# Three value products later, GpSimd for a VectorE iteration, and SyncE loads reordered, in a two-layer graph kernel

## The chip, the core and the metric

The kernel runs on one core of a Trainium2 chip. The time is device microseconds of one execution; the median of 12 executions before the change is 1186.02 us. The profiles used below each show one execution.

A core has five engines with queues of their own, each working in order: TensorE (PE; its weight loads are shown apart as PEld), VectorE (DVE), ScalarE (ACT), GpSimd (POOL) and SyncE (SP, which here only issues transfers). Transfers (DMA) are issued from SP's, ACT's or POOL's queue. An instruction that reads what another engine wrote waits on a semaphore, and all that is behind it on its engine waits too.

## The reference

`x` is 4096 x 512, `adj` a sparse symmetric 4096 x 4096 matrix with ones on the diagonal. Two layers follow each other:

```python
h = max(layernorm(x), 0)
Q, K, V = h @ WQ.T, h @ WK.T, h @ WV.T             # 8 heads of 64
attn = softmax(Q K^T / 8 + Q we^T + be, masked by adj)
hard = (attn == max of the row) / 8                # only the best neighbour(s) count
x = x + hard @ V

h = max(layernorm(x), 0)
agg = (mask @ h) / degree
x = x + relu(concat(h @ W_self + b_self, agg @ W_nb + b_nb) @ W_comb + b_comb)
```

## The kernel before the change, in words

Rows are worked in 32 tiles of 128. The kernel uses that a row has few neighbours: it makes lists of them, sorts the rows by degree, and gathers neighbours' keys and values from a table `K_d` in HBM whose row holds value, key, rank, neighbour list, layer-norm numbers and x. The order of instructions inside the stages is written out by hand: each engine's queue follows the program text.

**Stage 1** (a loop over tiles `t`, lines 955 to 1016, and what follows to 1105). In turn t the loop loads x for tile t+8 and the adjacency for tile t+2 (`load_adj`, two halves of 128 x 2048 int32, in a ring of seven half tiles: four in a pool, three in unused parts of the big tile `room`). GpSimd cuts out the diagonal block of tile t+1 (`no_self`, L673 and L677). ACT turns each half into a mask (L759) and takes row sums. PE packs the masks of tile t-1 into words by 17 small matmuls into one of two PSUM buffers `pw` (`pack`, L775 and L778), makes the keys of tile t (`keys`, four pairs of matmuls, L635) and, for tiles in `EARLY_V`, its values at once. DVE scales the keys of tile t-1 (L829, written to `K_d` by POOL at L834), finds the 24 largest words of tile t-2 (`words_top`, L849 to L853; it is what sets a `pw` free), takes row statistics of tile t+7, every fourth turn makes the reciprocal deviations of four tiles (`deviations`, L795 to L801, with `newton`, three rounds of four small instructions on DVE, L537 to L540) and in between decodes words into neighbour lists (`decode`, in pieces). Values made early are copied by ACT and written by POOL (`values_out`, L845 and L846), in the turn behind their product.

Values of the other tiles (`late_v`) are made later, from `room`, where the transposed rows are kept: eleven (`BESIDE`) beside the sorting and the last decoding (`more_values`), the rest in the first turn of stage 2 (L1674 to L1683). Zeros are written in `K_d` first where values come so late (L1024), and the x columns of half the rows are copied by four HBM-to-HBM transfers (L1019). Then SP loads the query weights `wq` into the buffer that held `wk` (L1025), biases, and the weights that are to be folded.

**Stage 2** (a loop over `turns`, L1649 on) does a tile of sorted rows in each turn. POOL gathers the rows themselves (`rows`, five turns ahead; tile `km`), then for each neighbour its key (`key_gathers`). The first 14 sorted tiles are `apart`: only keys are gathered (tiles `kg`, a ring of four groups of four), and the winner's value is gathered by head later (`o<-K_d,vi`, eight issues). The other 18 are `fused`: key and value are gathered together into `room`, so all values must be in `K_d` by then. `wide` fused rows gather their own value with `km` in one issue. DVE multiplies and sums queries and keys (L1243, L1249) and picks winners. Layer 1's products, the folding of weights (`fold`) and other work go in between. The planner's table `plan` gives the turn of each later step of a row from its place in `turns`.

**Stage 3** gathers layer 1's neighbour rows, multiplies the eight densest tiles as matrices, and writes the output.

Of the kernel before, what the change touches and what calls it, by code (L numbers as in the profile page):

```python
# [529 lines left out]
    nc.vector.bn_aggr(mv, st)  # L530


def newton(nc, pool, v, r, n, steps):

    c = pool.tile([P, n], F32, tag="nw_c", name="nw_c")
    for _ in range(steps):
        nc.vector.tensor_tensor(c, r, r, ALU.mult)  # L537
        nc.vector.tensor_tensor(c, c, v, ALU.mult)
        nc.vector.tensor_scalar(c, c, -0.5, 1.5, ALU.mult, ALU.add)
        nc.vector.tensor_tensor(r, r, c, ALU.mult)  # L540


@with_exitstack
def sparse_path(
# [40 lines left out]
    bb = cp.tile([P, D], F32, tag="sbb", name="sbb")  # L585
    wp = ctx.enter_context(tc.tile_pool(name="sw", bufs=1))

    EARLY_V = list(range(1, KT - 1, 2))
    late_v = [t for t in range(KT) if t not in EARLY_V]
    RING = 3  # L590
    SOON = 5
# [4 lines left out]
    def hT(t):  # L596
# [9 lines left out]
    END_R = HALF_R + (len(late_v) - SOON) * D  # L606
    spare = [
        room[:, at : at + N // 2]
        for at in (HALF_R - N, HALF_R - N // 2, END_R)
    ]  # L610
    assert (RING + SOON) * D <= HALF_R - N and END_R + N // 2 <= KT * D

    F = room[:, 0:HALF_R].rearrange("p (c f) -> p c f", f=D)

# [22 lines left out]
    with ExitStack() as pa:  # L637
# [18 lines left out]
        def load_adj(t):  # L656
            halves = []
            for j in range(2):
                k = (2 * t + j) % 7
                if k < 4:  # L660
                    at = a3.tile([P, N // 2], I32, tag="adjt", name="adjt")
                else:
                    at = spare[k - 4].bitcast(I32)
                nc.sync.dma_start(at, adj[ts(t, P), ts(j, N // 2)])
                halves.append(at)
            st[t]["adj"] = halves
# [124 lines left out]
        def deviations(t):  # L791

            mv = st[t]["mv"]
            v = ap.tile([P, XB], F32, tag="rs_v", name="rs_v")
            nc.vector.tensor_scalar(v, mv[:, :, 1], EPS, None, ALU.add)  # L795
            g = ap.tile([P, XB], I32, tag="rs_h", name="rs_h")
            nc.vector.tensor_scalar(g, v.bitcast(I32), 1, None, ALU.logical_shift_right)
            rs = meta[:, t : t + XB, M_LN]
            nc.vector.tensor_scalar(rs.bitcast(I32), g, -1.0, float(MAGIC), ALU.mult, ALU.add)
            newton(nc, ap, v, rs, XB, 3)  # L800
            nc.vector.scalar_tensor_tensor(  # L801
                meta[:, t : t + XB, M_LN + 1], mv[:, :, 0], -1.0, rs, ALU.mult, ALU.mult
            )
# [146 lines left out]
        def decode_some(n):  # L950
            for _ in range(n):
                next(decoding, None)

        FROM_X = KT // 2
        for t in range(KT):

            on(load_x, t + 2 * XB)
            on(load_adj, t + 2)
            if t < FROM_X:
                nc.sync.dma_start(K_d[ts(t, P), D + M_X : VKX], st[t]["x"])  # L960
            if t == 3:
                nc.scalar.dma_start(beb, be.rearrange("(o d) -> o d", o=1).to_broadcast([P, 1]))
            on(no_self, t + 1)
            on(masks, t, 0)
            on(turned_copy, t)
            on(masks, t, 1)
            on(of_self, t)
            on(norm, t + 1)
            if t == KT - 1:
                l3.close()  # L970
                rk = pa.enter_context(tc.tile_pool(name="srk", bufs=1))
                one = rk.tile([P, BINS * KT], F32, tag="r_one", name="r_one")
                nc.gpsimd.memset(one, 1.0)
                degc = rk.tile([P, KT], F32, tag="degc", name="degc")
                nc.vector.tensor_tensor(degc, degs[:, :, 0], degs[:, :, 1], ALU.add)
                rank = rk.tile([P, KT], I32, tag="rank", name="rank")
                nc.vector.tensor_scalar(rank, degc, float(BINS - 1), None, ALU.min)
                nc.vector.tensor_copy(degc, rank)
                oh = rk.tile([P, BINS, KT], BF16, tag="r_oh", name="r_oh")
                nc.vector.tensor_tensor(  # L980
                    oh, degc.unsqueeze(1).to_broadcast([P, BINS, KT]), binv, ALU.is_equal
                )
                tot = rk.tile([P, BINS * KT], F32, tag="r_tot", name="r_tot")
                acc = rk.tile([P, BINS * KT], F32, tag="r_acc", name="r_acc")
                ohf = oh.rearrange("p b t -> p (b t)")
                HF = BINS * KT // 2
            on(keys_out, t - 1)
            if t - 1 in EARLY_V:
                values_out(t - 1, st[t - 1]["pv"], ap, nc.gpsimd)
            on(pack, t - 1)  # L990
            on(keys, t)
            if t in EARLY_V:
                st[t]["pv"] = values(t, psm)
            on(turned, t + 1)
            if t == KT - 1:
                pts = [psm.tile([P, HF], F32, tag="pm", name="r_pt") for k in range(2)]
                for k in range(2):
                    nc.tensor.matmul(pts[k], onesb, ohf[:, ts(k, HF)], start=True, stop=True)
                    nc.scalar.copy(tot[:, ts(k, HF)], pts[k])
                pps = [psm.tile([P, HF], F32, tag="pm", name="r_pp") for k in range(2)]  # L1000
                nc.tensor.matmul(pps[0], tri, ohf[:, ts(0, HF)], start=True, stop=True)
            if t == 1:
                pads()
            if t == 5:
                tables()
            on(words_top, t - 2)
            on(stats, t + 2 * XB - 1)
            if t % XB == 0 and t + XB < KT:
                deviations(t + XB)
            if t - 1 in BATCHES[1:]:  # L1010
                if decoding:
                    decode_some(99)
                k = BATCHES.index(t - 1)
                decoding = decode(BATCHES[k - 1], BATCHES[k] - BATCHES[k - 1])
            if decoding and t < KT - 2:
                decode_some(2 if t < 28 else 4)
        for b in range(4):
            n = (KT - FROM_X) * P // 4
            nc.sync.dma_start(  # L1019
                K_d[ds(FROM_X * P + b * n, n), D + M_X : VKX], x[ds(FROM_X * P + b * n, n), :]  # L1020
            )

        for t in late_v[SOON:]:
            nc.sync.dma_start(K_d[ts(t, P), 0:D], zero)  # L1024
        load_w("wq", wqT, "w_a")  # L1025
        nc.sync.dma_start(bb, bcomb.rearrange("(o d) -> o d", o=1).to_broadcast([P, D]))
        for b, bias in zip(bcs, (bself, bnb)):
            nc.sync.dma_start(b, bias.rearrange("(c p) -> p c", p=P))
# [10 lines left out]
        def more_values(n):  # L1039
            make_values(n - len(made))  # L1040
            for t, pv in made:

                at = END_R + len(written) % 4 * D
                written.append(values_out(t, pv, None, nc.gpsimd, room[:, at : at + D]))
            made.clear()


# [62 lines left out]
    with ExitStack() as pb:  # L1110
# [343 lines left out]
        def fold(k, i):  # L1454

            pm = psm.tile([P, D], F32, tag="pm", name="pmw")
            if i < NC:
                left = F[:, ds(2 * k * NC, NC), ts(i, P)]
            else:
                left = fbs[k].rearrange("p (c q) -> p c q", q=P)  # L1460
            project(pm, left, F[:, ds((2 * k + 1) * NC, NC), :])
            if i < NC:
                nc.scalar.copy((wS, wN)[k][:, i, :], pm)
            else:
                biased.append(pm)

# [100 lines left out]

        fused, apart = list(range(VTILE, KT)), list(range(VTILE))
        last_tiles, ahead = fused[-4:], fused[-8:-4]
        turns = [r for pair in zip(apart, ahead + fused[:-8]) for r in pair] + last_tiles  # L1570
        pos = {r: p for p, r in enumerate(turns)}

        OWN0 = (LISTV - 1) * VK
        OWNS = (KT * D - OWN0) // VKX


        wide = [r for r in fused[:-8] if pos[r] > 12]
        big = room


# [68 lines left out]
        for i in range(-5, KT):  # L1649
# [9 lines left out]
            if i == KT - 1:  # L1659
                wT = wp.tile([P, DENSE, SEG + 2], I32, tag="w_a", name="wT")  # L1660
                nc.sync.dma_start(
                    wT[:, :, 0:SEG], W_d.rearrange("r p h q -> p r (h q)")
                )
            if i == 1:
                wS = wp.tile([P, NC, D], F32, tag="w_b", name="swS")
                wN = bp.tile([P, NC, D], F32, tag="swN", name="swN", bufs=1)
            a, b = on(key_gathers, i), late(value_gathers, "value", i)
            while a or b:
# [2 lines left out]
                        gather(*g)  # L1671
                    del q[:n]
            on(rows, i + 5)
            if i == 0:  # L1674
                for k, t in enumerate(late_v):
                    vs = xp.tile([P, D], F32, tag="xo", name="vs", bufs=2)
                    w = values_out(t, values(t, psm), None, nc.sync, vs)
                    for g in beyond:
                        tc.declare_no_dep(w.ins, g.ins, reason="other columns")
                    written.append(w)  # L1680
                    if k < 4:
                        ranks(turns[0], k, k + 1)
                late_v.clear()  # L1683
            words_copy()
            late(layer1_move, "move", i)
            on(query_copy, i + 2)
# [247 lines left out]
```

## Time and profile before

| what | value |
|---|---|
| median of 12 executions | 1186.02 us (1182.03 to 1189.09) |
| the profiled execution | 1183.13 us, its span 1181.4 us |
| mean granted TensorE clock | 0.932 |
| busy in the span: PE, DVE, ACT, POOL | 87%, 85%, 46%, 59% |
| bytes moved by DMA | 347.66 MB, mean 294 GB/s |
| stage 1, to the last decode on DVE | 303.3 us |
| stage 2, to the last key gather on POOL | 869 us |
| first row gather (`km`) | 307.75 us |
| first fused row gather | 355.21 us |

A timeline row of the profile gives start and length in us, engine, source line, operation, output and input tile, shape, how many; then in brackets the idle time of the engine ahead of it and what ended it. The table by stretches gives busy us and instruction counts of each engine for a stretch of the span. A group row gives busy us and mean ns of one instruction, then the idle time ahead. "issue" is time in which the engine waited for nothing that the profile shows. Ends of matmuls are modelled, so a full PE is not PE at its peak.

### The profile page before, as it was taken

The page shows a single profiled execution, that of the slowest core. Times are in us where ns is not written, and L with a number is a line of the kernel's source. Part 1 is how long each engine was busy: PE and PEld are TensorE (multiplying, and loading weights), DVE is VectorE, ACT ScalarE, POOL GpSimd, SP SyncE. Part 2 cuts the span into 40 slices and gives each one's busy share as a digit, 9 for nine tenths or more (in the row PEclk, how much of TensorE's full clock was granted, in tenths as well). Part 3 has the DMA queues.
Part 4 walks back from the last instruction along what each step waited for, and adds up shares of the span by engine and source line. Part 5 has one row for each costly group of instructions (what it writes and reads, how often), then busy time and mean ns, then how long its engine had stood idle before and what let it go on. Part 6 is the DMA issues. An engine that isn't in the chain of part 4 may idle for free.

```text
span 1181.4 us, 11445 instructions
## 1 busy us (share of the span) xinstructions
PE 1022.2 (87%) x3078; PEld 499.6 (42%) x3079; DVE 1000.8 (85%) x1652; ACT 549.1 (46%) x1222; POOL 695.2 (59%) x829
## 2 busy tenths in 40 slices
PE   4799999999589849976778988988989999999792
PEld 2455555554234324433334444434434444444340
DVE  6357989999388899989999999999993699998894
ACT  4577777771223358565667678845462100000000
POOL 1221222223557777777777777777713777777774
PEclk9899999999799979978889888988999999999996
DMA  9999999999587769888999888998865888988973
GB/s 352 419 419 419 383 413 400 355 341 252 192 229 231 249 210 316 259 262 287 287 289 296 275 287 286 293 287 277 287 249 178 303 304 276 319 288 275 373 244 109
DMA packets 114891, 347.66 MB, mean 294 GB/s; under 512 B 21408, under 2 KB 23488, under 8 KB 106624
## 3 DMA queue, kind: packets, MB, share of 16 engines
q0 software_dynamic: 60720, 201.79, 53.0%
q1 hardware_dynamic: 49696, 144.99, 32.0%
q10 hardware_dynamic: 4400, 0.05, 0.3%
q8 instruction: 26, 0.43, 0.1%
q14 instruction: 49, 0.40, 0.1%
HBM read 287.75 MB, written 63.21 MB: 297 GB/s over the span
## 4 chain that ended last, share of the span: by engine, by line
PE 26%; DMA 22%; DVE 21%; POOL 14%; issue 10%; ACT 4%; SPq 1%; POOLq 0%; DVEq 0%; ACTq 0%
POOL room L1120 8%; PE pk L635 7%; DMA room<-K_d,sidx 6%; DVE pr L1243 6%; PE pv L635 5%; DMA room<-G_d,sidx 5%; DVE sc L1249 4%; PE pw L778 3%; PE pr L1392 3%; PE pg L635 3%; POOL o L1120 2%; DMA K_d<-s 2%; PE q L635 2%; DVE acc L1825 2%; POOL out_dram L1136 2%
## 5 line engine op out<-in xcount | busy, mean ns | idle before, releaser
L1800 PE MATMUL da<-gk,mk 128*128 128x512 f32 x512 | 223.0, 598 | 7.2 <-DVE mk L1555 6.5
L1120 POOL DMA_INDIRECT room<-G_d,sidx x174 | 169.8, 976 | 84.5 <-issue 79.6
L635 PE MATMUL q<-wq,hqT 128*128 128x512 f32 x256 | 150.9, 744 | 57.6 <-DVE pr L1243 57.6
L1249 DVE TENSOR_REDUCE sc<-pr 128x32 f32<-128x2048 f32 (+3 forms) x114 | 183.3, 1608 | 3.8
L1120 POOL DMA_INDIRECT kg<-K_d,sidx x161 | 152.8, 949 | 48.9 <-issue 40.4
L1825 DVE TENSOR_REDUCE acc<-room 128x512 f32<-128x4096 f32 (+5 forms) x23 | 152.9, 6648 | 31.1 <-DMA room<-G_d,sidx 29.5
L1800 PEld LDWEIGHTS da<-gk,mk 128*128 128x128 f32 x512 | 98.2, 192 | 132.0 <-issue 122.9
L1120 POOL DMA_INDIRECT room<-K_d,sidx x118 | 111.4, 944 | 52.4 <-issue 20.7
L635 PE MATMUL pk<-wk,room 128*128 128x512 f32 x256 | 119.9, 613 | 9.4 <-ACT room L820 9.4
L1120 POOL DMA_INDIRECT o<-K_d,vi x112 | 107.0, 955 | 34.1 <-issue 32.6
L635 PEld LDWEIGHTS q<-wq,hqT 128*128 128x128 f32 x256 | 59.2, 243 | 129.4 <-issue 77.0
L635 PE MATMUL pv<-wv,room 128*128 128x512 f32 x256 | 112.9, 592 | 0.0
L1392 PE MATMUL pr<-swS,hT 128*128 128x512 f32 x216 | 99.1, 602 | 0.0
L1243 DVE TENSOR_TENSOR pr<-q,kg 128x2048 f32<-128x2048 f32 (+3 forms) x47 | 93.3, 1985 | 6.0 <-DMA kg<-K_d,sidx 4.9
L635 PE MATMUL pg<-swN,hT 128*128 128x512 f32 x216 | 97.1, 593 | 0.0
L1243 DVE TENSOR_TENSOR pr<-q,room 128x2048 f32<-128x2048 f32 (+3 forms) x43 | 73.9, 1718 | 15.6 <-DMA room<-K_d,sidx 12.7
L759 ACT ACTIVATE mkt<-adjt,sgb 128x2048 bf16<-128x2048 int32 x37 | 74.0, 2000 | 2.6 <-POOL adjt L677 2.6
L635 PEld LDWEIGHTS pv<-wv,room 128*128 128x128 f32 x256 | 48.4, 190 | 59.8 <-issue 59.8
L635 PEld LDWEIGHTS pk<-wk,room 128*128 128x128 f32 x256 | 47.9, 197 | 59.1 <-issue 48.7
L834 POOL DMA_DIRECT2D K_d<-ks x32 | 18.9, 589 | 79.9 <-DVE ks L829 76.6
L1392 PEld LDWEIGHTS pr<-swS,hT 128*128 128x128 f32 x216 | 41.8, 194 | 56.1 <-issue 55.2
L778 PE MATMUL pw<-mkt,planes 128*128 128x256 bf16 x512 | 61.1, 273 | 0.0
(254 smaller groups left out, 1638.2 us busy)
## 6 DMA issues: line engine op xcount, KB each, us to landing
adjt<-adj_dram SPq DMA_DIRECT2D x37, 1024.0 KB, 11.3
room<-adj_dram SPq DMA_DIRECT2D x27, 1024.0 KB, 12.2
x<-X_d SPq DMA_DIRECT2D x25, 512.0 KB, 7.8
xt<-x_dram SPq DMA_DIRECT2D x32, 256.0 KB, 8.1
K_d<-ks POOLq DMA_DIRECT2D x32, 256.0 KB, 6.5
X_d<-xo SPq DMA_DIRECT2D x32, 256.0 KB, 5.7
G_d<-gs SPq DMA_DIRECT2D x32, 256.0 KB, 4.5
gk<-G_d SPq DMA_DIRECT2D x16, 512.0 KB, 5.1
```

The costliest lines, as they stand in the source:

```text
L635: nc.tensor.matmul(dst, h[:, c, :], w[:, c, :], start=(c == 0), stop=(c == NC - 1))
L759: nc.scalar.activation(mk, st[t]["adj"][j], AF.Sigmoid, bias=sgb, scale=400.0, accum_out=degs[:, t, j : j + 1],)
L778: nc.tensor.matmul(pw, planes[:, s, :], st[t]["mk"][j][:, ts(i, SEG)], start=False, stop=(s == NPL - 1),)
L834: nc.gpsimd.dma_start(K_d[ts(t, P), D : 2 * D], ks)
L1120: last[0] = nc.gpsimd.indirect_dma_start(out=dst, out_offset=None, in_=src, in_offset=bass.IndirectOffsetOnAxis(ap=idx, axis=0), element_o ...
L1136: new = nc.gpsimd.indirect_dma_start(out=dst, out_offset=bass.IndirectOffsetOnAxis(ap=perm[:, r : r + 1], axis=0), in_=src, in_offset=None,)
L1243: nc.vector.tensor_tensor(pr[:, :g, :], s["q"].unsqueeze(1).to_broadcast([P, g, D]), kk[:, :, 0:D], ALU.mult)
L1249: nc.vector.tensor_reduce(sc[:, g0 : g0 + g, :], pr[:, :g, :].rearrange("p g (h d) -> p g h d", h=H), AX.X, ALU.add,)
L1392: nc.tensor.matmul(pr, s["hT1"][:, c, :], wS[:, c, :], start=False, stop=(c == NC - 1 and mine is None and not open_))
L1800: nc.tensor.matmul(dacc[r], masks[s][:, r, h, :], keys[s][:, h, :], start=(s == 0 and h == 0), stop=(s == NPL - 1 and h == 1),)
L1825: nc.vector.tensor_reduce(acc, g[:, 0:n, :].rearrange("p n f -> p f n"), AX.X, ALU.add)
```

## The change

It has six parts in one edit.

1. `newton` takes an engine, and `deviations` gives GpSimd: its twelve small instructions in each of eight calls leave DVE and stand in POOL's queue.
2. `EARLY_V` ends at tile 23 instead of 29: tiles 25, 27 and 29 join `late_v`, which has 20 tiles now instead of 17. Eleven are still made beside the sorting, six in turn 0 of stage 2 as before, and three in turn 1. Their rows in `room` take the place of the third spare half tile.
3. The adjacency ring has therefore six half tiles.
4. `wq` is loaded ahead of the four x copies and the zeros in SP's queue (there are 15 zeros instead of 12).
5. Late values beside the sorting are copied to four buffers in the pool `srk` instead of a part of `room`.
6. The first ten turns have another order: two `apart` tiles come ahead of the first `fused` one. The buffer for one folded weight is taken a turn later, with its copy order exchanged to suit, and `wide` begins two places later (7 rows instead of 8).

```diff
-def newton(nc, pool, v, r, n, steps):
+def newton(nc, pool, v, r, n, steps, eng=None):
+    eng = eng or nc.vector
     c = pool.tile([P, n], F32, tag="nw_c", name="nw_c")
     for _ in range(steps):
-        nc.vector.tensor_tensor(c, r, r, ALU.mult)
-        nc.vector.tensor_tensor(c, c, v, ALU.mult)
-        nc.vector.tensor_scalar(c, c, -0.5, 1.5, ALU.mult, ALU.add)
-        nc.vector.tensor_tensor(r, r, c, ALU.mult)
+        eng.tensor_tensor(c, r, r, ALU.mult)
+        eng.tensor_tensor(c, c, v, ALU.mult)
+        eng.tensor_scalar(c, c, -0.5, 1.5, ALU.mult, ALU.add)
+        eng.tensor_tensor(r, r, c, ALU.mult)
...
-    EARLY_V = list(range(1, KT - 1, 2))
+    EARLY_V = list(range(1, 24, 2))
...
-        for at in (HALF_R - N, HALF_R - N // 2, END_R)
+        for at in (HALF_R - N, HALF_R - N // 2)
...
-                k = (2 * t + j) % 7
+                k = (2 * t + j) % 6
...
-            newton(nc, ap, v, rs, XB, 3)
+            newton(nc, ap, v, rs, XB, 3, nc.gpsimd)
...
+        load_w("wq", wqT, "w_a")
         for b in range(4):
             n = (KT - FROM_X) * P // 4
             nc.sync.dma_start(
...
         for t in late_v[SOON:]:
             nc.sync.dma_start(K_d[ts(t, P), 0:D], zero)
-        load_w("wq", wqT, "w_a")
...
-                at = END_R + len(written) % 4 * D
-                written.append(values_out(t, pv, None, nc.gpsimd, room[:, at : at + D]))
+                vs = rk.tile([P, D], F32, tag="vs", name="vs", bufs=4)
+                written.append(values_out(t, pv, None, nc.gpsimd, vs))
...
-                nc.scalar.copy((wS, wN)[k][:, i, :], pm)
+                nc.scalar.copy((wN if k else wS)[:, i, :], pm)
...
-        turns = [r for pair in zip(apart, ahead + fused[:-8]) for r in pair] + last_tiles
+        turns = [apart[0], apart[1], ahead[0], apart[2], ahead[1], apart[3], ahead[2], fused[0]]
+        turns += [apart[4], ahead[3]]
+        turns += [r for pair in zip(apart[5:], fused[1:-8]) for r in pair] + last_tiles
...
-        wide = [r for r in fused[:-8] if pos[r] > 12]
+        wide = [r for r in fused[:-8] if pos[r] > 14]
...
+            if i == 2:
+                wS = wp.tile([P, NC, D], F32, tag="w_b", name="swS")
             if i == 1:
-                wS = wp.tile([P, NC, D], F32, tag="w_b", name="swS")
                 wN = bp.tile([P, NC, D], F32, tag="swN", name="swN", bufs=1)
...
-            if i == 0:
-                for k, t in enumerate(late_v):
+            if i in (0, 1):
+                n = 6 if i == 0 else len(late_v)
+                for k, t in enumerate(late_v[:n]):
                     vs = xp.tile([P, D], F32, tag="xo", name="vs", bufs=2)
                     w = values_out(t, values(t, psm), None, nc.sync, vs)
...
-                    if k < 4:
+                    if k < 4 and i == 0:
                         ranks(turns[0], k, k + 1)
-                late_v.clear()
+                del late_v[:n]
```

Line numbers in the text are those of the kernel before; the changed kernel's are one higher from L537 on, and a little more in stage 2.

More of the change, by code (lines that the diff above doesn't have):

```diff
@@ L608, in sparse_path @@
         room[:, at : at + N // 2]
-        for at in (HALF_R - N, HALF_R - N // 2, END_R)
+        for at in (HALF_R - N, HALF_R - N // 2)
     ]
-    assert (RING + SOON) * D <= HALF_R - N and END_R + N // 2 <= KT * D
+    assert (RING + SOON) * D <= HALF_R - N and END_R <= KT * D
     F = room[:, 0:HALF_R].rearrange("p (c f) -> p c f", f=D)
```

## The prediction

> **What bounds the kernel now.** I read the table of busy time by stretches first, then the timelines of VectorE, GpSimd and TensorE one by one, and the chain of waits last. Columns of the first view: stretch, its length, busy us (instructions) of PE, PEld, DVE, ACT, POOL, granted clock, DMA share, GB/s.
>
> ```profile
> 135.00:150.00 15.00, 15.00 (x67) 8.66 (x66) 14.14 (x44) 11.79 (x18) 6.68 (x13) 1.00 0.90 347
> 240.00:255.00 15.00, 15.00 (x67) 8.68 (x66) 13.80 (x61) 11.79 (x19) 5.43 (x11) 1.00 1.05 379
> 600.00:700.00 100.00, 83.03 (x228) 39.86 (x227) 96.01 (x119) 76.16 (x201) 75.60 (x81) 0.88 0.90 290
> ```
>
> Stage 1 (adjacency, keys, values; to about 303 us) shows two full engines: PE 15.00 of 15, and DVE 13.8 to 14.1, which with some 0.03 us between its many small instructions is also full. PE goes in steps of exactly 14.89 us for two tiles, and the chain of waits runs through it there, so at first PE looks like the bound. The timelines of DVE, PE and POOL say which has room:
>
> ```profile
> 116.85 0.17 DVE L795 TENSOR_SCALAR rs_v<-mv 128x4 f32<-128x4 f32 x1
> 119.86 0.17 DVE L801 SCALAR_TENSOR_TENSOR meta<-mv,meta 128x4 f32<-128x4 f32 x1
> 136.45 0.41 DVE L850 MATCH_REPLACE8 w<-top,pw 128x256 f32<-128x256 f32 x1
> 166.84 0.69 DVE L829 SCALAR_TENSOR_TENSOR ks<-pk,swe 128x512 f32<-128x512 f32 x1 [2.81 <-PE pk L635]
> ...
> 137.29 0.27 PE L775 MATMUL pw<-jrow,sidb 128*128 128x256 bf16 x1
> 257.04 0.27 PE L775 MATMUL pw<-jrow,sidb 128*128 128x256 bf16 x1 [0.46 <-DVE w L850]
> ...
> 121.32 0.54 POOL L846 DMA_DIRECT2D K_d<-vs  x1 [6.74 <-ACT vs L845]
> 143.35 0.22 POOL L926 TENSOR_TENSOR meta<-slot,selfs 128x8 f32<-128x8 f32 x1
> 143.66 0.27 POOL L927 TENSOR_SCALAR meta<-meta 128x8 f32<-128x8 f32 x1
> 144.01 0.88 POOL L930 TENSOR_SCALAR meta<-meta 128x192 f32<-128x192 f32 x1
> ```
>
> From 107.3 to 258.4 DVE has one idle time over 0.3 us, the 2.81 us before 166.84. From 166.84 to the last decoding at 303.3 it has only one more, 1.1 us at 258.4. PE's step at 137.29 starts 0.43 us after DVE let go of its PSUM buffer at 136.86, it is again 0.43 us at 196.85, and at 257.04 PE waits for DVE. So DVE sets the end of stage 1, and PE has no room against it either.
>
> Stage 2 (scores and winners, to about 869 us) is set by GpSimd: 81 gather issues in 100 us, 0.95 us each and 0.30 behind each, or 1.25 us apart. From 316 to 855 us POOL makes a break of over half a us only once:
>
> ```profile
> 345.03 0.94 POOL L1120 DMA_INDIRECT km<-K_d,perm  x1 [0.30 <-issue]
> 355.21 0.94 POOL L1120 DMA_INDIRECT room<-K_d,sidx  x1 [9.24 <-DMA K_d<-vs]
> 356.46 0.94 POOL L1120 DMA_INDIRECT room<-K_d,sidx  x1 [0.30 <-issue]
> ```
>
> The first fused row's gathers wait there until the last late value has landed. What delays POOL's first gather moves the end, and what fills this break gains.
>
> **The change, part by part.**
>
> 1. *The iteration on GpSimd.* Twelve instructions, 0.20 us apart on DVE (2.4 us), leave DVE in each of eight calls. But the next DVE instruction (L801, L802 in the new kernel) reads their result, and in the instruction order of the changed kernel it stands directly behind L800. DVE, which works in order, stands still meanwhile: nothing is taken off it unless GpSimd is faster. GpSimd's nearest rows are L926 and L927, 0.31 and 0.35 us apart: 9 x 0.31 + 3 x 0.34 = 3.8 us, and about 0.3 us to hand over. Bounds: 2.4 us (DVE's own pace) and 5.4 us (L927's longest, 0.44, for every step).
>
> The page "GPSIMD Engine Reference", section 4.1 of the Trainium skill, gives elementwise work to VectorE because two-input operations are about twice as slow on GPSIMD. Its measured 1.96 (section 3.1, 2048 columns) would make 4.7 us of the twelve, and the sum 2.7 us more than mine. That is an estimate. L926 at 0.22 against DVE's 0.17 speaks for less at this size.
>
> There is a second wait. In POOL's new order the iteration stands behind the issue of the values of tile t-1 (L846), which waits for ACT. At tile 12 DVE arrives at 116.85, POOL is through with that issue only at 121.87. I follow DVE's lateness from call to call:
>
> - Calls at 4 and 8 fall where DVE still has idle time (gaps of 5.35 and 3.21 us behind them). 0.6 us remain. The call ahead of the loop now waits for the first adjacency tile (POOL's select at 13.54), and makes ACT's first mask some 5 us late. POOL's break until 42.99, for the pads' write, swallows that; without it, 5 us more.
> - Tile 12: 121.87 + 3.8 + 0.3 = 126.0 against 120.0: 5.9 late. PE's step at 137.29 has 0.43 of room: PE, and with it ACT and the values' issue, 5.5 late.
> - Tile 16: the issue ends at 151.65 + 5.5, DVE goes on at 161.3 against 152.6: 8.7 late, less the gap of 2.8 before 166.84: 5.9.
> - Tile 20: 181.43 + 5.5 + 4.1 = 191.0 against 179.6: 11.4 late, PE 11.0 (room 0.43 at 196.85).
> - Tile 24: POOL is ready. 4.1 + 0.1 instead of 2.4: 13.2 late.
>
> The gap of 1.1 us at 258.4 closes, so stage 1's DVE work ends **12.1 us later** (with the bounds of 2.4 and 5.4 us: 8 and 17).
>
> 2. *Three values late.* PE loses 3 x 3.44 = 10.3 us in tiles 25, 27 and 29. DVE keeps all its instructions there and is the bound, so this is worth 0 in stage 1. If DVE had room, up to 10.3.
>
> 3. *Adjacency ring of 6 halves instead of 7.* Each load waits for a mask one later, 2.5 to 5 us. Tile 5's block landed at 54.48 and its mask started at 61.36; later odd tiles have 7.6 to 10 us. I take 0; cover gone, the excess is paid each tile.
>
> 4. *Query weights ahead of x copies and zeros.* On SP, in order, the load waits for the last key product (262.3 now, some 275.5 then), and behind it stand four x copies, 15 zeros (three more) and the weights of the fold, which were issued from 233.18 on. That block took 26.3 us, from 233.18 to 259.5; three more zeros at 1.4 us make 30.5, to some 306. Their first reader is the row gather at some 325. I take 0. The weights are read at 318.8 now, so an earlier load gains nothing.
>
> 5. *Late values' buffers in another pool.* The first row gather now waits for all eleven late writes, and its semaphores in the new instruction list say so. Before, it went at 307.75, between writes 9 and 10. Without the gathers in between, the eleventh issue ends about 309.1 in old times and lands 2.8 (write 7) to 5.5 us (median) later, so the gather is 4 to 6.5 us later: **+5**. Then five go without a break, and the first key gather starts 7.3 instead of 8.5 us behind the first: **-1.2**.
>
> 6. *The first ten turns.* POOL now issues 23 + 1 + 14 + 1 gathers ahead of the first fused row instead of 23 + 1. From the first row gather that is 7.3 + 39 x 1.25 = 56 us. PE: first query product done 15.4 after that gather, six values (20.6), a query product (3.4), three values (10.3): 50; copy and write as before, 0.6 + 5 to 8.6: 55.6 to 59. So of the wait of 9.24 us about 2 remain (0 to 5): **-7.2**. Fused row 2 is no longer wide and gathers its own values apart, one issue: **+1.25**. From turn 10 on the order is the same.
>
> Sum against the profiled execution (1183.13 us, span 1181.4): 12.1 + 5 - 1.2 - 7.2 + 1.25 = +10. That run lies 2.9 below the median of 1186.0. Forecast **1196 us**.
>
> **Rivals.**
>
> *A. VectorE is not the bound (faster).* PE's exact step and the chain through it speak for this. Then the 10.3 us pay, and with the -2.2 of parts 5 and 6 it is -12.5: 1173.5. It decides if the wait for GpSimd is under the 2.4 us it replaces plus DVE's real slack. Against it: the 2.81 us gap is the only one in 150 us.
>
> *B. The iteration costs what it frees* (no change): DVE arrives late anyway, GpSimd keeps 0.2 us. Then -2.2: 1184. Against it: 121.87 is set by ACT.
>
> *C. The shorter ring starves the masks* (slower still): for it, POOL waits 33.1 us for adjacency loads in all. Missing 0.4 us a tile in some 25 tiles: 10 more, 1206.
>
> *D. The x copies and zeros end behind the row gather.* Taking twice the 26.3 us, they end near 335 instead of 325: 1206. For it: eleven values, a later start and the fold's weights share the DMA then. Against it: less than half its bandwidth was used (121 GB/s from 285 to 300 us).
>
> **How the numbers follow.** Forecast 0.66 (own range 1189 to 1203, from the bounds 8 to 17 and 0 to 5), A 0.08, B 0.07, C 0.10, D 0.09. About 0.2% (2.4 us) is what a measurement can tell from no change. Slower 0.66 + 0.10 + 0.09 = 0.85, same 0.07, faster 0.08. The range reaches from B's edge to D's: 1185 to 1207, and leaves out A and what lies beyond.
>
> **What would show it.** Right: twelve GpSimd instructions 0.3 us apart, and behind each set an idle time of DVE before L802, of 4 to 8 us; TensorE waiting for DVE near tiles 14 and 22; the last decode's write of meta near 316 instead of 303.9; the first row gather some 17 us later; POOL's break at the first fused row down to some 2 us. Wrong: DVE through with the decoding before 304, masks waiting for adjacency loads, or the row gather waiting for SP's transfers.

## The result, and the profile after

The changed kernel takes **1209.91 us** (median of 8 runs, 1208.46 to 1214.30) beside 1186.02 us: a ratio of 1.0208, 95% interval 1.0195 to 1.0222. It is slower, as forecast, but by 24 us and not by 10: outside the range (1185 to 1207). The profiled execution took 1211.09 us, its span is 1209.4 us (before 1183.13 and 1181.4). Six kernels of the experiments were first run where the kernel before itself took 1472 us (values3_all, before_rows4, pool_to_end, after_both, both and after_three); five of them were run again where it took its usual time, and it is those runs (_2) that are read.

The busy time by stretches, with the columns as before; the last two rows are new.

```profile
135.00:150.00 15.00, 11.35 (x35) 5.86 (x33) 14.14 (x46) 5.76 (x8) 6.13 (x13) 0.77 1.00 399
240.00:255.00 15.00, 12.27 (x63) 7.46 (x62) 13.94 (x55) 11.76 (x18) 5.41 (x11) 1.00 0.66 244
600.00:700.00 100.00, 81.61 (x226) 39.69 (x225) 91.52 (x114) 64.30 (x172) 75.78 (x80) 0.85 0.90 289
...
285.00:300.00 15.00, 14.36 (x64) 6.71 (x63) 14.17 (x41) 2.56 (x4) 2.77 (x5) 1.00 1.05 389
300.00:315.00 15.00, 15.00 (x36) 6.63 (x36) 12.37 (x59) 3.03 (x6) 5.99 (x11) 1.00 1.12 222
```

In the two stretches of stage 1 PE is busy for 11.35 and 12.27 us where it was full. DVE is busy there for as much as before (its long waits, below, fall between these stretches): DVE holds up the others. From 600 us on GpSimd issues at its old pace. From 285 to 300 us the DMA engines moved 121 GB/s before and 389 now.

DVE at tile 12, and what GpSimd does meanwhile (timelines: start, length, idle time before it and who ended it):

```profile
113.82 0.17 DVE L800 TENSOR_SCALAR meta<-rs_h 128x4 int32<-128x4 int32 x1
121.77 0.22 DVE L802 SCALAR_TENSOR_TENSOR meta<-mv,meta 128x4 f32<-128x4 f32 x1 [7.78 <-POOL meta L541]
...
117.88 0.54 POOL L847 DMA_DIRECT2D K_d<-vs  x1 [4.34 <-ACT vs L846]
118.44 0.21 POOL L538 TENSOR_TENSOR nw_c<-meta 128x4 f32<-128x4 f32 x1
...
121.53 0.20 POOL L541 TENSOR_TENSOR meta<-meta,nw_c 128x4 f32<-128x4 f32 x1
```

Twelve GpSimd instructions, 0.28 us apart, start when the issue of the values (L847) has had its wait for ACT. DVE stands still for 7.78 us over both. It waits so in each of the six calls of the loop: 6.05, 7.77, 7.78, 7.56, 7.78 and 3.41 us.

GpSimd from the end of stage 1 on: first the last write of meta and the first row gather before; then, in the changed kernel, the same two, the issue of the last late value between them, and every later break of over half a us ahead of a gather up to 880 us:

```profile
303.88 0.95 POOL L932 DMA_DIRECT2D K_d<-meta  x1 [10.50 <-issue]
307.75 1.07 POOL L1120 DMA_INDIRECT km<-K_d,perm  x1 [0.51 <-issue]
...
314.13 0.95 POOL L933 DMA_DIRECT2D K_d<-meta  x1 [8.30 <-DMA bc<-L_gnn_b_self_dram]
318.79 0.54 POOL L847 DMA_DIRECT2D K_d<-vs  x1 [0.45 <-ACT vs L846]
327.81 1.06 POOL L1121 DMA_INDIRECT km<-K_d,perm  x1 [8.48 <-DMA K_d<-vs]
...
384.25 0.94 POOL L1121 DMA_INDIRECT room<-K_d,sidx  x1 [0.79 <-PE pmw L636]
...
445.78 0.94 POOL L1121 DMA_INDIRECT km<-K_d,perm  x1 [6.81 <-DVE xo L1318]
538.72 0.94 POOL L1121 DMA_INDIRECT km<-K_d,perm  x1 [8.35 <-DVE xo L1318]
```

The last write of meta starts 0.55 us behind DVE's last instruction of the decoding in before and in after, whatever the bracket names. The break of 9.24 us at the first fused row is down to 0.79. The two at the end are new: the gather of rows into a tile `km` waits until DVE has added up layer 1 (`xo`) of an earlier row. The difference of the two profiled executions, along GpSimd's queue:

| place | before | after | difference |
|---|---|---|---|
| last write of meta | 303.88 | 314.13 | +10.25 |
| from there to the first row gather | 3.87 | 13.68 | +9.8 |
| from there to the first key gather | 8.5 | 7.2 | -1.3 |
| break at the first fused row | 9.24 | 0.79 | -8.45 |
| one more issue (row 16) | | | +1.25 |
| breaks ahead of two row tiles (0.30 each is usual; 6.81 + 8.35 now) | 0.60 | 15.16 | +14.6 |
| sum | | | +26.2 |
| last gather of stage 2 | 868.99 | 896.27 | +27.3 |

What the table leaves open is 1 us, and behind the last gather of stage 2 the kernel takes 313.1 us where it took 312.4. The 28.0 us between these two executions are 23.9 between the medians: that of before lies 2.9 us under its median, that of after 1.2 over its own.

### The profile page after: what moved, and what is told of

It is laid out like the page before. It is cut to its first block, busy times and chain, and to the rows that moved or that the text cites. A ratio compares the mean times of both kernels' runs of the same rounds, so it can differ in the third digit from the quotient of the medians.

```text
span 1209.4 us, 11436 instructions
## 1 busy us (share of the span) xinstructions
PE 1026.7 (85%) x3079; PEld 502.8 (42%) x3079; DVE 982.3 (81%) x1556; ACT 550.2 (45%) x1222; POOL 713.6 (59%) x923
## 4 chain that ended last, share of the span: by engine, by line
DVE 27%; PE 23%; DMA 19%; POOL 15%; issue 10%; ACT 5%; POOLq 0%; DVEq 0%; SPq 0%; ACTq 0%
POOL room L1121 8%; DVE pr L1244 6%; PE pk L636 5%; PE pv L636 5%; DVE sc L1250 5%; DMA room<-K_d,sidx 5%; DMA room<-G_d,sidx 4%; DMA kg<-K_d,sidx 3%; PE pw L779 3%; PE pr L1393 3%; POOL o L1121 2%; PE pg L636 2%; DVE acc L1830 2%; DVE o L1290 2%; POOL kg L1121 2%
## 5 line engine op out<-in xcount | busy, mean ns | idle before, releaser
L636 PE MATMUL q<-wq,hqT 128*128 128x512 f32 x256 | 147.8, 731 | 50.8 <-DVE pr L1244 50.8
L760 ACT ACTIVATE mkt<-adjt,sgb 128x2048 bf16<-128x2048 int32 x44 | 88.0, 2000 | 6.9 <-PE pw L779 4.1
L779 PE MATMUL pw<-mkt,planes 128*128 128x256 bf16 x512 | 65.8, 285 | 0.0
L779 PEld LDWEIGHTS <-planes 128*128 128x128 bf16 x512 | 52.2, 102 | 28.3 <-issue 20.3
```

The costliest lines, as they stand in the source:

```text
L636: nc.tensor.matmul(dst, h[:, c, :], w[:, c, :], start=(c == 0), stop=(c == NC - 1))
L760: nc.scalar.activation(mk, st[t]["adj"][j], AF.Sigmoid, bias=sgb, scale=400.0, accum_out=degs[:, t, j : j + 1],)
L779: nc.tensor.matmul(pw, planes[:, s, :], st[t]["mk"][j][:, ts(i, SEG)], start=False, stop=(s == NPL - 1),)
```

## Experiments

My theory after this reading: the iteration costs the 10 us by which stage 1 ends later, the two new waits for row tiles cost 15 and come from the new order of turns alone, and the rest lies in what the first row gather waits for. The rival for each part stands in its expectation. Times are medians; each ratio is to the kernel before, run on the same chip beside it, with its 95% interval. Where two kernels were run on different chips, the ratios compare them better than the medians.

### The iteration

**vec_newton**, the changed kernel with one edit, and **pool_newton**, the kernel before with the opposite one:

```diff
-            newton(nc, ap, v, rs, XB, 3, nc.gpsimd)
+            newton(nc, ap, v, rs, XB, 3)
```

> The changed kernel with the deviations' iteration back on VectorE, nothing else undone. Theory (the iteration is worth the whole of what the last meta write moved, 303.9 to 314.1 us): the six idle stretches of VectorE ahead of L802 go, the last meta write is issued near 304, and the time falls by 8 to 11 us, to 1199-1202. Rival (the first row gather waits for the long SP transfers that now start behind the last key product, at whatever time VectorE ends): the meta write moves as much, but the first row gather stays within 5 us of 327.8 and the time falls by less than 5 us, to 1205-1210.

> The kernel before with the deviations' iteration on GpSimd, nothing else of the change. Theory (VectorE stands still behind GpSimd, in order, and it bounds the first stage): the last meta write moves from 303.9 to 313-315 us and the time rises by 9 to 11 us, to 1195-1197. Rival (the kernel before has room elsewhere, and the idle time on VectorE shows in the changed kernel only because of its other edits): the time stays within 3 us, 1183-1189.

The last write of meta in vec_newton, then in pool_newton:

```profile
303.03 0.95 POOL L933 DMA_DIRECT2D K_d<-meta  x1 [8.65 <-DMA bc<-L_gnn_b_self_dram]
...
314.60 0.95 POOL L933 DMA_DIRECT2D K_d<-meta  x1 [10.50 <-issue]
```

Measured: vec_newton 1200.21 us (1.0119, 1.0096 to 1.0141), 9.7 under the changed kernel; its last write of meta is at 303.03, its first row gather at 316.40. pool_newton 1196.79 us (1.0087, 1.0069 to 1.0104), 10.3 over the kernel before; its last write of meta is at 314.60. The iteration costs 10 us, alone or among the other edits, and both rivals fall.

**pool_to_end**, the kernel before with the iteration on GpSimd, and the product behind it there too:

```diff
-            nc.vector.scalar_tensor_tensor(
-                meta[:, t : t + XB, M_LN + 1], mv[:, :, 0], -1.0, rs, ALU.mult, ALU.mult
-            )
+            nb = meta[:, t : t + XB, M_LN + 1]
+            nc.gpsimd.tensor_tensor(nb, mv[:, :, 0], rs, ALU.mult)
+            nc.gpsimd.tensor_scalar(nb, nb, -1.0, None, ALU.mult)
```

> The kernel before with the iteration and the product behind it (as two instructions) on GpSimd, so that VectorE has nothing to wait for there; nothing else of the change. Theory (VectorE bounds the first stage, and the iteration cost time only because VectorE stood behind it): the idle time ahead of L802 is gone, VectorE has six times some 2.6 us less to do, and the time falls by 5 to 13 us, to 1173-1181. Rival (another engine bounds as closely, or ScalarE's norm waits for GpSimd in place of VectorE): within 3 us of before, 1183-1189.

> As pool_to_end, on another chip: 1173-1181 if VectorE bounds the first stage at the usual clock; within 3 us of before if another engine bounds as closely.

Measured (_2): 1182.04 us beside 1186.53 (0.9962, 0.9949 to 0.9975). DVE's timeline of pool_to_end_2 at the same tile:

```profile
113.72 0.17 DVE L800 TENSOR_SCALAR meta<-rs_h 128x4 int32<-128x4 int32 x1
113.80 0.26 DVE L850 MAX8 d_lf<-d_cand 128x8 f32<-128x96 f32 x1
```

DVE goes straight on to the decoding, while GpSimd does the same twelve instructions at the same time (118.26 to 121.55). So the 10 us were DVE's waiting, not GpSimd's pace. The gain, 4.5 us (3.0 to 6.1), lies just under what the theory gave: DVE's decoding ends at 299.73, only 3.6 us earlier, although some 14 us of work left DVE. From 30 to 300 us DVE now waits 38.6 us for TensorE's key products (32.3 before) and once (4.79 us at 255.9) for ScalarE. So other engines are close behind, as the rival had it in part.

### The order of the turns

**turns_only**, the kernel before with the new `turns`, `pos[r] > 14`, and what belongs to them (the late values over two turns, `w_b` reused a turn later):

> The kernel before with the changed order of the turns alone: two plain rows first, fused row 2 (row 16) in the ring of row tiles, w_b's reuse a turn later. Theory (with two plain rows first the second freed row tile comes a turn later, while row tiles are issued in the same turns, so GpSimd waits for layer 1's sum): two GpSimd breaks ahead of a row gather, together 8 to 16 us, both ended by VectorE's xo; the break at the first fused row shrinks from 9.2 to about 1 us; the sum is 0 to +9 us, 1186-1195. Rival (the prediction's: from turn 10 on the order is the same and nothing else waits): -6 us, 1180, with no new break.

Measured: 1193.99 us (1.0058, 1.0041 to 1.0074), 7.5 over the kernel before. The break at the first fused row is under 1 us, and both new ones are there, in GpSimd's timeline of turns_only:

```profile
427.95 0.94 POOL L1120 DMA_INDIRECT km<-K_d,perm  x1 [6.69 <-DVE xo L1317]
...
520.97 0.93 POOL L1120 DMA_INDIRECT km<-K_d,perm  x1 [8.40 <-DVE xo L1317]
```

Where they come from can be counted. Row tiles share eight buffers, each free again when its row's sum has been made, so row tile n waits for the sum that is number n - 8 in order of time; it is issued five turns ahead of its own turn. DVE's sums and GpSimd's tenth row tile, in before:

```profile
378.13 0.69 DVE L1317 TENSOR_TENSOR xo<-km,o 128x512 f32<-128x512 f32 x1
399.45 0.69 DVE L1317 TENSOR_TENSOR xo<-km,o 128x512 f32<-128x512 f32 x1
...
430.74 0.95 POOL L1120 DMA_INDIRECT km<-K_d,perm  x1 [0.30 <-DVE q L1347]
```

and in after:

```profile
411.86 0.68 DVE L1318 TENSOR_TENSOR xo<-km,o 128x512 f32<-128x512 f32 x1
...
437.41 1.48 DVE L1473 TENSOR_TENSOR sbb<-pmw,sbb 128x512 f32<-128x512 f32 x2
...
444.82 0.69 DVE L1318 TENSOR_TENSOR xo<-km,o 128x512 f32<-128x512 f32 x1
...
537.77 0.68 DVE L1318 TENSOR_TENSOR xo<-km,o 128x512 f32<-128x512 f32 x1
```

Before, the second sum is done at 400.1, over 30 us ahead of the tenth tile. There the second turn is a fused row, whose winners need no second gather, so its sum comes early (turn 2), and row 0's in turn 3. Now turn 1 is a plain row as well. The first sum comes in turn 3, the second in turn 4, behind the two biases' sum on DVE (L1473 to L1481, 437.41 to 444.0), and GpSimd reaches the tenth tile at 438.97. The second break is the fifteenth tile, at the row of position 14. In before that row had the fourteenth tile, because row 16 was wide; now row 16 takes one too, and the fifteenth needs the seventh sum (537.77 in the lines above), which ends at 538.45 while GpSimd stands ready at 530.37.

**turns_rows4**, turns_only with row tiles from position 9 on issued a turn later; **before_rows4** is the same edit in the kernel before:

```diff
-            on(rows, i + 5)
+            if i != 4:
+                on(rows, i + (5 if i < 4 else 4))
```

> The kernel with the changed order of the turns alone (1193.99 us), and the row tiles of position 9 and later issued four turns ahead instead of five, so that each stands on GpSimd one turn behind the sum that gives up its buffer. Theory (the two waits for a freed row tile, 6.69 and 8.41 us, are what the order costs): both go, and the time falls by 11 to 15 us, to 1179-1183, under the kernel before. Rival (GpSimd and VectorE are both nearly full in these turns, so that GpSimd's waits only show VectorE's lag): GpSimd waits elsewhere for VectorE, and the time falls by less than 5 us, to 1189-1194.

> The kernel before with the row tiles of position 9 and later issued four turns ahead, the order of the turns as it was: a control. Theory (the waits for freed row tiles belong to the changed order; before, the freed tile was there 5 to 30 us ahead): no gain, 1184-1189. Rival (issuing row tiles later is worth something in any order): 5 us or more, 1180 or less.

> As before_rows4, on another chip: within 2 us of before if the waits for freed row tiles belong to the changed order, 5 us or more under it if later row tiles are worth something in any order (the run at the low clock was 0.55% under before, which speaks for some of it).

Measured: turns_rows4 1177.21 us beside 1184.87 (0.9932, 0.9914 to 0.9951), some 15 us less than turns_only by the ratios. Between 353 and 620 us GpSimd has no break of over 0.7 us. The tenth tile of turns_rows4 is issued 10 us behind the second sum:

```profile
427.37 0.69 DVE L1317 TENSOR_TENSOR xo<-km,o 128x512 f32<-128x512 f32 x1
...
438.16 0.94 POOL L1120 DMA_INDIRECT km<-K_d,perm  x1 [0.30 <-DVE o L1289]
```

before_rows4_2 takes 1184.80 us beside 1186.53 (0.9989, 0.9978 to 1.0000): at most a little. So the two waits cost what they last, and belong to the new order. With them gone, the order is worth 8 us.

**turns_bias4**, turns_only with the biases' sum a turn later:

```diff
-            3: [(1, NC), (0, NC)],
+            4: [(1, NC), (0, NC)],
```

> The kernel with the changed order of the turns alone (1193.99 us), and the sum of the two biases (7.4 us on VectorE right ahead of the second freed row tile) a turn later. Theory (each wait for a freed row tile is a chain of its own: VectorE's work ahead of that sum): the first break, 6.69 us, goes and the second stays, the time falls by 5 to 7 us, to 1187-1189. Rival (VectorE's lag is what counts, and only its place moves): the first break goes, the second grows by as much, and the time stays within 2 us of 1194.

Measured: 1189.56 us beside 1184.87 (1.0050, 1.0032 to 1.0067), not told apart from turns_only. Neither expectation was met as it stood: the tenth tile waits 0.38 us, as good as nothing, but the eleventh waits 5.80 us for the third sum, which now has the biases' sum ahead of it, and the second break is still 7.54 us. The first wait follows the biases' sum; put off by a turn, the sum moves the wait and hardly shortens it.

### The weights' load and the late values

**wq_behind**, the changed kernel with `load_w("wq", ...)` back behind the x copies and zeros:

> The changed kernel with the query weights' load put back behind the last x copies and zeros, nothing else undone. Theory (the load waits for the last key product to give up its buffer, and SP's queue stands behind it, so 8 MB of x copies and zeros that could start near 255 us start near 277 and slow the late value writes that the first row gather waits for): the copies start by 260 us, the last late write lands within 6 us instead of 9, the first row gather comes 3 to 8 us earlier than 327.8, and the time falls by 3 to 8 us, to 1202-1207. Rival (the prediction's: the place of the load costs nothing): within 2 us of 1209.9.

Measured: 1206.03 us (1.0155, 1.0138 to 1.0172), 4 us less by the medians and 6 by the ratios. SP's timeline of after, then of wq_behind:

```profile
274.37 0.38 SPq L630 DMA_DIRECT2D wq<-L_gnn_WQ_dram  x1
274.80 5.69 SPq L1021 DMA_DIRECT2D K_d<-x_dram  x4
280.53 20.55 SPq L1026 DMA_DIRECT2D K_d<-s  x15
```

```profile
243.36 6.71 SPq L1020 DMA_DIRECT2D K_d<-x_dram  x4
250.12 19.71 SPq L1025 DMA_DIRECT2D K_d<-s  x15
274.94 0.38 SPq L630 DMA_DIRECT2D wq<-L_gnn_WQ_dram  x1
```

With the load ahead of them, the copies wait for the last key product (the load's buffer) and start 31 us later. The last late write is then issued at 318.79 and the row gather goes 9.0 us later; in wq_behind it is issued at 319.97 and the gather goes 3.3 us later. The gather of wq_behind, and the stretch in which it falls, in after and then in wq_behind:

```profile
323.29 1.06 POOL L1121 DMA_INDIRECT km<-K_d,perm  x1 [2.77 <-DMA K_d<-vs]
```

```profile
315.00:330.00 15.00, 2.15 (x6) 0.61 (x4) 1.17 (x8) 0.60 (x1) 5.06 (x9) 0.74 0.94 317
315.00:330.00 15.00, 2.30 (x8) 0.99 (x7) 1.17 (x8) 1.72 (x4) 9.45 (x15) 0.66 0.60 201
```

From 320 to 325 us, when the last late write is under way, the DMA engines move 105 GB/s in wq_behind in place of 358, with a DMA share of 0.27 in place of 1.01, and the late writes issued from 295 to 330 us land after 2.9 us (median) in place of 8.3. What moves then in after is no longer the copies and zeros, whose last issue ends at 301.1, but what stands behind them on SP: loads of the weights to be folded, 1 MB each, which SP issues up to 318.4 us in after and up to 296.6 in wq_behind. That they slow the writes by sharing the DMA engines is the likeliest reading; the run shows that the place of the load costs this, and not where on their way the transfers meet.

**values3** and **values3_all**: the changed kernel without its iteration, its load and its order, that is, three more late values, the ring of six halves and the late values' own buffers. In values3 the second stage's late values stay split over turns 0 and 1; under the old order the first fused row's gathers then stand ahead of the last three writes, so it reads values that are not written yet.

> The changed kernel with the iteration on VectorE, the query weights' load behind the copies and zeros, and the old order of turns: three more late values, the ring of six halves, and buffers of the late values outside the room are what is left. Theory (the first row gather now stands behind all eleven late writes): it comes 3 to 6 us later than 307.8 and the time is 1188-1192. Rival (the three values taken out of the first stage are worth something there, or the writes are hidden): the meta write comes ahead of 303 and the time is at or under 1186.

> The changed kernel with the iteration on VectorE, the query weights' load behind the copies and zeros, the old order of turns, and all late values of the second stage in turn 0 as before: three more late values, the ring of six halves and the late values' own buffers are what is left. Theory (the first row gather stands behind all eleven late writes): it comes 3 to 6 us later than 307.8; the time is 1188-1193. Rival (three values fewer are worth something to the first stage): the meta write comes ahead of 301 and the time is at or under 1185.

> As values3_all, on another chip: 1188-1193 if the first row gather stands 3 to 6 us behind the eleven late writes, at or under 1185 if three values fewer are worth something to the first stage.

Measured: values3 1206.57 us, 20 us of it one wait of GpSimd for the three writes: it tells of the split, not of the values. values3_all_2 1192.04 us beside 1186.53 (1.0057, 1.0040 to 1.0074), 5.5 over. Its last write of meta is at 303.35, so three values fewer and a shorter ring change next to nothing together at stage 1's end, 0.5 us (which of the two may give and which take was not tried). Its first row gather is at 311.45, 3.7 us later. And the break at the first fused row grows from 9.24 to 13.92 us; the new order hides that in the changed kernel.

### Together

**after_both** is the changed kernel with the edits of pool_to_end and turns_rows4, **after_three** has that of wq_behind too. **both** is the kernel before with the new order and the two edits of after_both.

> The changed kernel with two mends: row tiles of position 9 and later four turns ahead, and the product behind the iteration on GpSimd as well. Theory (the two GpSimd waits, 15.2 us, and VectorE's wait, 10 us, are independent): 23 to 32 us less, 1178-1187. Rival (the first row gather waits for the late writes and SP's transfers whenever VectorE ends): 15 to 19 us less, 1191-1195.

> As after_both, on another chip: 1178-1187 if the two waits are independent, 1191-1195 if the first row gather waits for writes and transfers whenever VectorE ends.

> The changed kernel with three mends: row tiles four turns ahead, the product on GpSimd, and the query weights' load behind the copies and zeros. Theory (the first row gather waits 6.7 us for late writes whose transfers share the queues with SP's): 3 to 5 us under the two mends' 1180.0, so 1175-1177. Rival (the writes wait for ScalarE, not for transfers, once VectorE stands still nowhere): 1179-1181.

> The kernel before with the changed order of turns, row tiles of position 9 and later four turns ahead, and the iteration with its product wholly on GpSimd; the number of late values, the ring of seven halves and the query weights' place as before. Theory (the gains of the parts add: 7.7 us of the order with its mend, 4.5 us of the iteration): 1173-1176. Rival (the break at the first fused row, which the order hides, comes back when the first stage ends earlier): 1178-1182.

> As after_three, on another chip: 1175-1177 if the place of the query weights' load still costs its 4 us beside the other two mends (1180.0 without this one), 1179-1181 if it costs nothing any more.

Measured: after_both_2 1180.02 us beside 1186.53 (0.9939, 0.9920 to 0.9957), 30 under the changed kernel. after_three_2 **1172.03 us** beside 1185.30 (0.9895, 0.9878 to 0.9911): faster than both kernels, by 13 and 38 us. It is under what was expected, and the reason shows in GpSimd's timelines of after_both_2 and of after_three_2, which differ by the place of the load alone:

```profile
296.76 0.93 POOL L933 DMA_DIRECT2D K_d<-meta  x1 [8.33 <-DMA bc<-L_gnn_b_self_dram]
313.38 1.06 POOL L1121 DMA_INDIRECT km<-K_d,perm  x1 [6.71 <-DMA K_d<-vs]
...
296.11 0.93 POOL L933 DMA_DIRECT2D K_d<-meta  x1 [10.23 <-issue]
304.13 1.06 POOL L1121 DMA_INDIRECT km<-K_d,perm  x1 [2.81 <-DMA K_d<-vs]
```

The last write of meta comes within 0.7 us of the same time, but the first row gather 9.25 us earlier: with the first stage shorter, the place of the load costs twice as much at that gather as in the changed kernel (4.5 us), and 5 us of the whole time by the ratios, 8 by the medians.

In these two kernels the last write of meta also comes 7 to 8 us ahead of before. DVE's decoding is through at 295.55 in after_three_2, against 299.73 in pool_to_end_2. Of what differs between these two, the three values fewer on TensorE are the likeliest to give these 4 us, now that DVE no longer waits for GpSimd; they were not tried alone. The kernel **both** was not run again: beside the 1472 us its ratio is 0.9944 (0.9910 to 0.9977), which says no more than that it gains.

## Why the prediction was right in its sign and wrong in its size

- **Part 1, the iteration: right.** +12.1 forecast, +10.25 on the last write of meta, 9.7 and 10.3 us in the two runs. The idle time before L802, the twelve instructions (3.3 us against 3.8 forecast, and 0.04 us, 121.73 to 121.77, to hand the result over, against 0.3) and TensorE waiting for DVE at tiles 14 and 22 are there (3.65 us each, ahead of 138.89 and 206.30). On the way the sums were 1.6 to 4 us too high: DVE comes to the reader of the iteration (L801, now L802) 1.9 us late at tile 12 where 5.9 was forecast, because the issue of the values, ahead in GpSimd's queue, came at 117.88 and not at 121.32; at tiles 16, 20 and 24 it is 7.0, 9.8 and 10.9 us late (8.7, 11.4 and 13.2 forecast). DVE's six waits add up to 40.4 us. Only a quarter of it is paid: 14 us of work left DVE, and its waits for the key products fell from 32.3 to 16.7 us (from 30 to 300 us). The page "GPSIMD Engine Reference" of the Trainium skill (section 3.1) has a ratio of 1.96 for a large two-input operation; here, on 4 columns, GpSimd's pitch of 0.28 us against DVE's 0.20 is 1.4, so the measurement decides against the 4.7 us worked out from the page.
- **Parts 2 and 3, late values and ring: right.** 0 at the end of stage 1, as values3_all_2 shows for both together. The "if DVE had room" of part 2 is the likeliest source of the 4 us in after_three_2. Rival C, the starved masks, read its row too low: GpSimd's waits for adjacency loads before are 33.1 us for the half tiles in the pool and 18.0 more for those in `room`. In after they are 32.5 and 17.1, and the rival did not come about.
- **Part 4, the weights' load: wrong.** "I take 0", because the transfers were put at an end near 306 and the first reader at 325. What counts is not the row gather as their reader: the late writes, for which that gather waits, land later while the block's last loads are moving. Measured 4 to 6 us here, more in after_three_2. Rival D had the place, and named the fold's weights among its reasons, but its point of decision (the copies ending behind the gather) was not the one: SP issues the last zeros by 301.1 us, and the gather goes at 327.81.
- **Part 5, the late values' buffers: right.** +5 forecast; the first row gather comes 3.7 us later in values3_all_2. In wq_behind the last meta write and the first row gather are 8.05 us apart, against 3.87 before: 4.2. -1.2 forecast for the five gathers in a row, -1.3 found.
- **Part 6, the turns: the failed step.** The break at the first fused row went as said (-7.2 forecast, -8.45 found), and so did row 16's extra issue. But the step took the break it removes for the only wait that the new order touches: "From turn 10 on the order is the same." That is true of the order and not of the times. By the planner the first five sums of layer 1 come a turn later, one more row takes a row tile, and the row tiles are issued as early as ever. The two waits for them, 15.16 us, were in no term and in no rival. The wait for a buffer's release was in the kernel to be read (`bufs=8`, `rows` five turns ahead, `xo` at the planned turn), and the trace of before had the 30 us of room ahead of the tenth tile that were used up.

With 15 more for part 6 and 5 for part 4 the sum of +10 becomes +30, against +28.0 between the profiled executions; the 2 us are about what part 1 was forecast too high.

## What to carry to other kernels

When work is reordered, list every buffer ring whose allocation and release lie in the moved stretch, and compare for each the turn of the release with the turn of the next use: a ring that never made anybody wait has only as much room as the trace shows. Moving a small computation to another engine freed nothing here while the first engine's next instruction read its result; move the reader too, or put work between. A load put ahead in a queue makes everything behind it wait for that load's own buffer, and transfers that come late can cost through other writes under way at the time, not only through their own readers.

## What was not expected of the hardware

Where the kernel before took 1472 us, the first stage took as long as elsewhere (pool_to_end's first row gather is at 304.24 us, pool_to_end_2's at 304.27). The loss lay behind it. In all six traces taken there ScalarE stands still 23 to 27 times, for 254 to 308 us in all, in waits for which the profile names no instruction and no transfer, only "remote"; VectorE has 5 to 8 such waits. The other fourteen traces have none, and the loss is some 286 us. Many of the long waits of TensorE and VectorE there are put down to ScalarE. The longest wait is in ScalarE's timeline of the kernel **both**; the product that it copies had ended on TensorE at 370.87.

```profile
390.80 1.56 ACT L1464 COPY swN<-pmw 128x512 f32<-128x512 f32 x3 [31.98 <-remote]
```

The granted clock of that run is 0.86 over the span, but 1.00 from 150 to 250 us, and from 370.9 to 390 us TensorE has no work at all, so a slower TensorE is not what ScalarE waits for in that place. What held ScalarE is open. Nor is it shown that the loss belongs to a chip: on chip 15 the kernel before took 1184.87 us beside turns_rows4 and, half an hour later, 1472.90 us beside **both**.
